# Scores in pieces of 32 columns, one projection per unit, and a reordered tail in a recurrent-then-attention kernel

## The chip, the cores and the metric

The kernel runs on one core of one Trainium2 chip, in one launch. Its metric is device time in microseconds (us), the median of several executions; beside it there is one profiled execution, from which every instruction's start and duration come. A core has a matrix engine (TensorE, PE in the profile, with its weight loads as PEld), a vector engine (VectorE, DVE), a scalar engine (ScalarE, ACT), GpSimd (POOL), and a queue engine (SyncE, SP). They run side by side and wait for one another through semaphores; DMA transfers are issued from SP, POOL and ACT.

## The reference

`x` is (2, 2048, 256), float32. Two layers are added to it, each on the layer-normalised input.

```python
# layer 1: a recurrence over time
xi = layernorm(x) @ Wi.T + bi
h_t = tanh(xi_t + h_(t-1) @ Wh.T + bh)          # 2048 steps, width 256
x = x + h
# layer 2: attention with gated experts, H = 8 heads of DH = 64, E = 5 experts, 2 selected
y  = layernorm(x)
q, k = y @ Wq, y @ Wk                             # per head 2048 x 64
wv = topk_mask(y @ Ws, 2) * sigmoid(y @ Ws)       # which experts make v, with weights
v  = einsum('bthe,btek->bhtk', wv, y @ Wv)
attn = softmax(q @ k.T / 8) @ v                   # 2048 x 2048 scores for each batch and head
out = einsum('bthe,bthk,ekd->btd', topk_mask(y @ Wd, 2), attn, Wo)
x = x + out
```

Sixteen attention heads (2 batches of 8) are computed, each with 2048 x 2048 scores. All of it is float32. A float32 matmul of the program appears in the profile as two weight loads and two matmuls, called its two passes below.

## The kernel before

**Stages.** The recurrence takes the first 130 us. What follows is attention, from about 131 us to 1542 us, and a tail that `drain` writes out by hand, to 1604 us.

**Units and tiles.** `heads` lists 16 pairs (batch, head). A head is worked on in four *units* of QB = 512 queries (n = 0 to 3; `units` lists all 64). The 2048 keys of a head are 8 tiles, and a tile `t` of scores holds 2 x 128 keys by 512 queries in PSUM, two banks (`ps_s`, two buffers). The main loop runs over T; each T makes the scores of two new tiles, so a unit has U_T = 4 values of T, a head 16, and all of attention NT = 256. Products and sums of a tile follow LAG = 6 values of T later.

**One T.** The order is written out in the main loop: `exponential` of an old tile, `scores` of the two new tiles, `stage` (ACT copies a tile to SBUF), `largest` (DVE keeps the running maximum), `subtract` (the maximum is taken off, mostly by POOL, for the first tiles of a unit by DVE), the functions listed for this T in the table `before`, `products` of two old tiles (PE: exponentials times v), in some T `sums` (PE: column sums of the exponentials, with a matrix of ones), `exponential`, and the functions in the table `behind`. `fold` adds one tile to another with an accumulating DMA from POOL. Every engine works through its instructions in this order.

**Array tiles on PE.** `scores` (L635) multiplies 64 rows by 128 columns of `k` with 512 queries; its two matmuls, for o = 0 and o = 1, use the upper and the lower 64 rows of the array and write different PSUM banks, so they can run together. `products` (L715), `sums` (L736), `keys` (L140), `queries` (L159) and `project_out` (L868) use pieces of 32 columns by all 128 rows, four of which cover the array. Transposes (`turn_max`, `spread_max`, `weigh`, `turn_out`) use the whole array.

**Projections.** `keys(i, part)` and `queries(i, part)` project y to half of the keys or queries of head i: 8 matmuls (16 passes) into one PSUM buffer of the pool `misc` (two buffers), an ACT copy (L148) or scaling (L169), and for queries two DMAs on SP's queue that swap halves (L170, L171). A head needs four of them. With T0 = 16 i the first T of head i, they are put into `before` at

```python
at(before, T0 - 2 * U_T + 2, keys, i, 0)      # the head before, unit n = 2, its third T
at(before, T0 - 2 * U_T + 3, queries, i, 0)   # the head before, unit n = 2, its fourth T
at(before, T0 - U_T + 2, keys, i, 1)          # the head before, unit n = 3
at(before, T0 + 2, queries, i, 1)             # the head's own unit n = 0
```

so unit n = 2 has two projections, n = 3 and n = 0 one each, and n = 1 none. They stand between the scores and the products of their T.

**The end of a unit.** `take` (ACT L751, DVE L752) empties the single PSUM buffer `o` that `products` fills; `take_sums` does it for `d`. `close` weighs by the mask of experts, and `gather` adds the result in DRAM (`yd`). After the last head of a batch `fetch_y` brings a unit's sum back to SBUF (640 KB, SP's queue; two buffers `y`), `turn_out` transposes a block of 128 rows of it on PE and loads the residual `z` from DRAM (L860, SP's queue, three buffers), and `project_out` multiplies with Wo into a buffer `pz`, adds `z` on DVE (L876) and stores the block (L877, SP's queue).

**The tail.** In `drain` the last three units (w, v, u) are finished with the remaining blocks interleaved by hand: `turn()` and `project()` call `turn_out` and `project_out` for the next block. When it starts, the PSUM of the scores has been given to a pool of four buffers that `other` hands out; `turn_out` and `spread_max` use it there, `weigh` and `project_out` use `misc`. `close_last` ends the last unit, block by block.

Of the kernel before, what the change touches and what calls it, by code (L numbers as in the profile page):

```python
# [14 lines left out]
P = 128  # L15
# [5 lines left out]
def rnn_then_switchhead_kernel(  # L21
# [15 lines left out]
    nc = tc.nc  # L37
    B, T, D = x.shape
    E, _, DH = Wv.shape
# [80 lines left out]
    def misc(shape, nm):  # L120
        return ps_m.tile(shape, F32, tag="m", name=nm)
# [3 lines left out]
    k_of, q_of = {}, {}  # L125
# [431 lines left out]
    U_T = NCH // 4  # L557
# [71 lines left out]
    def scores(t):  # L629
        i, n = units[t // HC]  # L630
        c = t % HC
        ss = ps_s.tile([P, 2, QB], F32, tag="s", name=f"s{t}")
        for o in range(2):
            half = slice(o * DH, (o + 1) * DH)
            nc.tensor.matmul(  # L635
                ss[:, o, :],
                lhsT=k_of[i][half, c, :],
                rhs=q_of[i, n][o][half, :],
                start=True,
                stop=True,  # L640
            )
        return ss

    def stage(t, ss):
# [23 lines left out]
    def other(nm):  # L668
        return spare["pool"].tile([P, QB], F32, tag="z", name=nm)
# [8 lines left out]
    def reduce_max(u):  # L678
        pm, mq = mx_of[u]
        nc.vector.tensor_reduce(mq, pm, AX.X, ALU.max)  # L680
# [16 lines left out]
    def subtract(t, on_vector=False):  # L697
        u, c = t // HC, t % HC
        p = ring[t]
        on_vector |= c < 2  # L700
        eng, top = (nc.vector, top_of[u][0]) if on_vector else (nc.gpsimd, top_of[u][1])
        eng.tensor_tensor(p, p, top.unsqueeze(1).to_broadcast([P, 2, QB]), ALU.subtract)  # L702
# [4 lines left out]
    def products(t):  # L707
        u, c = t // HC, t % HC
        i, _ = units[u]
        if c == 0:  # L710
            o_of[u] = ps_o.tile([P, QB], F32, tag="o", name=f"o{u}")
        for o in range(2):
            for g in range(0, DH, 32):
                at_col = o * DH + g
                nc.tensor.matmul(  # L715
                    o_of[u][at_col : at_col + 32, :],
                    lhsT=v_of[i][:, 2 * c + o, g : g + 32],
                    rhs=ring[t][:, o, :],
                    start=c == 0,
                    stop=c == HC - 1,  # L720
                    tile_position=(0, at_col),
                )

    def fold(t):


        nc.gpsimd.dma_start(out=ring[t], in_=ring.pop(t + 1), accum_op=ALU.add)  # L727
# [69 lines left out]
    def fetch_y(u):  # L797

        i, n = units[u]
        b, _ = heads[i]  # L800
        y_of[b, n] = four.tile([P, QS, E, DH], F32, tag="y", bufs=2, name=f"y{b}_{n}")
        nc.sync.dma_start(out=y_of[b, n], in_=yd[b, n])

    def close_last(u, outs):

        i, n = units[u]
        b, _ = heads[i]
        po, mr = weigh(u)
        y = y_of[b, n]
        pr = four.tile([P, QS, E, DH], F32, tag="pro", bufs=1, name=f"pro{u}")  # L810
        def ready(s):
            masked(pr[:, s : s + 1], po, mr, s, 1)
            nc.vector.tensor_tensor(y[:, s], y[:, s], pr[:, s], ALU.add)

        ready(0)
        project_out(*outs[0])
        ready(1)
        project_out(*outs[1])
        for s in range(QS):
            turn_out(*outs[2 + s])  # L820
            if s + 2 < QS:
                ready(s + 2)
            if s:
                project_out(*outs[1 + s])
        project_out(*outs[-1])

    def gather(u):

# [31 lines left out]
        nc.sync.dma_start(out=z, in_=x1d[c, :, b, :])  # L860
        yT_of[b, c] = (yT, z)

    def project_out(b, c):
        yT, z = yT_of.pop((b, c))
        pz = misc([P, D], f"pz{b}_{c}")
        for k, (r0, m) in enumerate(o_chunks):
            for g in range(0, P, 32):
                nc.tensor.matmul(  # L868
                    pz[g : g + 32],
                    lhsT=yT[:, k, g : g + 32],  # L870
                    rhs=wo[:, k, :],
                    start=k == 0,
                    stop=k == len(o_chunks) - 1,
                    tile_position=(0, g),
                )
        nc.vector.tensor_tensor(z, pz, z, ALU.add)  # L876
        nc.sync.dma_start(out=out[b].rearrange("(n s) d -> s n d", s=NCH)[c], in_=z)  # L877
# [59 lines left out]
    before, first_behind, behind = {}, {}, {}  # L937

    def at(table, T, f, *a):
        table.setdefault(T, []).append(lambda: f(*a))  # L940
# [9 lines left out]
    for i, (b, h) in enumerate(heads):  # L950
        T0 = i * H_T
        if i == 0:
            at(before, 0, keys, 0, 1)
            for c in range(NCH):
                at(behind, (c + 2) // 3, first_experts, c)
        else:
            at(before, T0 - 2 * U_T + 2, keys, i, 0)
            at(before, T0 - 2 * U_T + 3, queries, i, 0)
            at(before, T0 - U_T + 2, keys, i, 1)
        at(before, T0 + 2, queries, i, 1)  # L960
        for part in range(4):
            if i == 0:
                at(behind, (3, 5, 6, 7)[part], mix, i, part)
                at(behind, (3, 5, 6, 7)[part], mix_sum, i, part)
            else:
                T = T0 + U_T * (part - 2) + 2
                at(behind, T - 2, fetch, i, part)
                at(behind, T, mix, i, part)
                at(before, T + 1, mix_sum, i, part)
        if h == H - 3 and b + 1 < B:  # L970
            for c in range(NCH):
                T = T0 + c // 2 * U_T + 1
                at(before if c % 2 else behind, T + c % 2, experts, b + 1, c)
    for b in range(1, B):

        T0 = (b - 1) * H * H_T + 2 * LAG + 3
# [22 lines left out]
    for u, (i, n) in enumerate(units):  # L999
        b, h = heads[i]  # L1000
# [3 lines left out]
        outs = [(b, n * QS + s) for s in range(QS)]  # L1004
# [19 lines left out]
    def drain():  # L1024


        w, v, u = len(units) - 3, len(units) - 2, len(units) - 1
        tv, tu = HC * v, HC * u
        outs = [(B - 1, c) for c in range(NCH)]
        turned, projected = 2, 1  # L1030

        def turn(n=1):
            nonlocal turned
            for _ in range(n):
                turn_out(*outs[turned])
                turned += 1

        def project(n=1):
            nonlocal projected
            for _ in range(n):  # L1040
                project_out(*outs[projected])
                projected += 1

        spread_max(v)
        turn_max(u)
        subtract(tv + 6, True)
        subtract(tv + 7)
        reduce_max(u)
        take_sums(w)
        exponential(tv + 5)  # L1050
        project()
        spread_max(u)
        products(tv + 4)
        products(tv + 5)
        fold(tv + 2)
        fold(tv + 4)
        exponential(tv + 6)
        exponential(tv + 7)
        subtract(tu, True)
        close(w)  # L1060
        gather(w)
        turn()
        fetch_y(v)
        exponential(tu)
        subtract(tu + 1, True)
        exponential(tu + 1)
        subtract(tu + 7)
        subtract(tu + 2, True)
        products(tv + 6)
        products(tv + 7)  # L1070
        fold(tv + 6)
        turn()
        project()
        take(v)
        sums(tv, tv + 2, True, False)
        project()
        exponential(tu + 2)
        subtract(tu + 3, True)
        exponential(tu + 3)
        subtract(tu + 4, True)  # L1080
        products(tu)
        products(tu + 1)
        turn()
        fold(tu)
        subtract(tu + 5, True)
        exponential(tu + 4)
        turn()
        project()
        products(tu + 2)
        products(tu + 3)  # L1090
        fold(tu + 2)
        sums(tv + 4, tv + 6, False, True)
        take_sums(v)
        exponential(tu + 5)
        subtract(tu + 6, True)
        turn()
        project()
        exponential(tu + 6)
        products(tu + 4)
        products(tu + 5)  # L1100
        exponential(tu + 7)
        turn()
        fetch_y(u)
        project()
        close(v)
        gather(v)
        products(tu + 6)
        products(tu + 7)
        take(u)
        project()  # L1110
        sums(tu, tu + 2, True, False)
        sums(tu + 4, tu + 5, False, False)
        sums(tu + 6, tu + 7, False, True)
        take_sums(u)
        turn()
        turn()
        project()
        turn()
        project()
        turn()  # L1120
        close_last(u, outs[-QS - 2 :])

    with tc.manual_schedule():
        for T in range(NT):
# [11 lines left out]
            ss = [scores(t) for t in new]  # L1136
# [84 lines left out]
```

## Time and profile before

| what | value |
|---|---|
| time, median of 3 | 1605.14 us (1604.32 to 1608.18) |
| the profiled execution | 1606.15 us, of which the span from the first to the last instruction is 1604.4 us |
| granted TensorE clock | 0.997 |
| PE busy | 1536.7 us, 96% |
| DVE, POOL, ACT busy | 1300.1, 1278.1, 1250.1 us (81%, 80%, 78%) |
| scores, L635 (two groups side by side) | 512.2 us each |
| products, L715 | 492.6 us |
| sums, L736 | 150.8 us |
| queries and keys, L159 and L140 | 63.3 and 61.5 us |
| DVE `largest`, L656 | 390.6 and 78.3 us |
| POOL `subtract`, L702 | 1046.6 us |

How to read it: a busy PE is not yet a PE at its peak, since a matmul's span covers its way through the array, and matmuls overlap. What a stage costs on PE is the distance from one pass's start to the next one's. Matmuls on different tiles of the array show as several records that start within hundredths of a microsecond. A wait names the engine whose signal came last. The shares are averages; what bounds a unit is read from that unit.

### The profile page before, as it was taken

How to read it: one execution, taken by the hardware profiler on the slowest of the kernel's cores; microseconds unless marked ns; L12 is line 12 of the kernel's file. 1: busy time of each engine (PE TensorE's matmuls, PEld its weight loads, DVE VectorE, ACT ScalarE, POOL GpSimd, SP SyncE). 2: the span in 40 equal slices, each digit the busy share in tenths (PEclk: the TensorE clock that was granted, in tenths of full speed). 3: DMA queues.
4: the chain of work that ended last, by engine and by line, in shares of the span. 5: the costliest groups of instructions: out<-in, count | busy, mean ns of one | idle time of the engine just before them, and what ended most of it. 6: DMA issues, size and time to landing. Idle time of an engine off the chain costs nothing.

```text
span 1604.4 us, 29221 instructions
## 1 busy us (share of the span) xinstructions
PE 1536.7 (96%) x11438; PEld 592.6 (37%) x11438; DVE 1300.1 (81%) x1811; ACT 1250.1 (78%) x1617; POOL 1278.1 (80%) x855
## 2 busy tenths in 40 slices
PE   7989899999999999999999999999999999999998
PEld 5974233333333333333333333333333333333233
DVE  7473889998988888888987769898889888898874
ACT  4664688888878888887877768888888888888873
POOL 3054699888888988999998768898889899888880
PEclk9999999999999999999999999999999999999999
DMA  5021468788888888788887757788888888789864
GB/s 163 1 107 31 114 151 195 162 186 178 174 164 173 171 178 174 154 176 176 166 186 163 166 137 178 173 174 173 170 166 168 173 165 180 155 171 178 177 140 128
DMA packets 86911, 253.30 MB, mean 158 GB/s; under 512 B 11952, under 2 KB 31216, under 8 KB 86768
## 3 DMA queue, kind: packets, MB, share of 16 engines
q0 software_dynamic: 43488, 164.65, 54.9%
q1 hardware_dynamic: 41648, 86.13, 17.5%
q8 instruction: 91, 1.49, 0.4%
q10 hardware_dynamic: 1632, 0.61, 0.2%
q14 instruction: 52, 0.43, 0.1%
HBM read 59.46 MB, written 50.33 MB: 68 GB/s over the span
## 4 chain that ended last, share of the span: by engine, by line
PE 67%; DVE 13%; DMA 5%; ACT 3%; issue 2%; POOL 2%; SPq 0%; DVEq 0%; ACTq 0%; POOLq 0%
PE s L635 23%; PE o L715 20%; PE d L736 6%; DVE m L656 5%; DMA p<-p 4%; PE pk L140 4%; PE pq L159 3%; PE pz L868 2%; ACT p L646 2%; DVE pro L781 2%; PE pt L689 2%; PE pm L675 1%; DVE p L702 1%; POOL p L702 1%; PE po L768 1%
## 5 line engine op out<-in xcount | busy, mean ns | idle before, releaser
L702 POOL TENSOR_TENSOR p<-p,top 128x1024 f32<-128x1024 f32 x378 | 1046.6, 3007 | 11.5 <-ACT top L695 11.4
L646 ACT COPY p<-s 128x1024 f32<-128x1024 f32 x512 | 511.1, 1012 | 150.9 <-DVE m L656 69.2
L705 ACT ACTIVATE p<-p 128x1024 f32<-128x1024 f32 x512 | 538.1, 1062 | 51.0 <-DVE p L702 39.7
L635 PE MATMUL s<-qs,k 64*128 64x512 f32 x1024 | 512.2, 618 | 6.3 <-ACT p L646 6.2
L635 PE MATMUL s<-q,k 64*128 64x512 f32 x1024 | 512.2, 618 | 3.2 <-ACT p L646 3.2
L715 PE MATMUL o<-p,v 128*32 128x512 f32 x4096 | 492.6, 598 | 9.9 <-DVE os L752 8.0
L656 DVE TENSOR_TENSOR m<-s,m 128x1024 f32<-128x1024 f32 x320 | 390.6, 1221 | 95.2 <-PE s L635 86.5
L727 POOL DMA_DIRECT2D p<-p x254 | 337.3, 1329 | 69.5 <-PE o L715 21.6
L715 PEld LDWEIGHTS o<-p,v 128*32 128x32 f32 x4096 | 113.9, 109 | 298.2 <-issue 157.6
L635 PEld LDWEIGHTS s<-qs,k 64*128 64x128 f32 x1024 | 168.9, 185 | 144.7 <-ACT p L646 47.8
L635 PEld LDWEIGHTS s<-q,k 64*128 64x128 f32 x1024 | 168.9, 185 | 137.5 <-issue 52.5
L736 PE MATMUL d<-p,ones 128*32 128x512 f32 x1032 | 150.8, 593 | 5.9 <-DMA p<-p 5.8
L702 DVE TENSOR_TENSOR p<-p,pt 128x1024 f32<-128x1024 f32 x126 | 152.3, 1209 | 0.0
L656 DVE TENSOR_TENSOR m<-s,p 128x1024 f32<-128x1024 f32 x64 | 78.3, 1224 | 55.9 <-ACT p L646 55.5
L835 POOL DMA_DIRECT2D yd<-pro x48 | 45.0, 937 | 92.7 <-DVE pro L781 90.4
L781 DVE TENSOR_TENSOR pro<-po,mr 128x1280 f32<-128x1280 f32 (+1 forms) x67 | 95.9, 1431 | 2.7
L620 DVE TENSOR_TENSOR xq<-xq,wp 128x1280 f32<-128x1280 f32 x60 | 89.2, 1487 | 2.3 <-DVE wp L618 0.2
L626 DVE TENSOR_REDUCE v<-xq 128x256 f32<-128x1280 f32 x60 | 88.5, 1476 | 0.0
L736 PEld LDWEIGHTS d<-p,ones 128*32 128x32 f32 x1032 | 36.9, 110 | 96.2 <-issue 76.4
L159 PE MATMUL pq<-xn2T,wq 128*32 128x512 f32 x512 | 63.3, 612 | 6.4 <-DVE rtd L427 6.4
L140 PE MATMUL pk<-xn2T,wk 128*32 128x512 f32 x512 | 61.5, 598 | 0.0
L680 DVE TENSOR_REDUCE mq<-pm 128x4 f32<-128x512 f32 x64 | 44.3, 692 | 18.3 <-PE pm L675 16.9
(179 smaller groups left out, 1480.9 us busy)
## 6 DMA issues: line engine op xcount, KB each, us to landing
p<-p POOLq DMA_DIRECT2D x254, 512.0 KB, 6.1
xq<-xvd SPq DMA_DIRECT2D x60, 640.0 KB, 5.5
yd<-pro POOLq DMA_DIRECT2D x48, 640.0 KB, 7.2
qs<-q SPq DMA_DIRECT2D x64, 128.0 KB, 2.6
yd<-pro SPq DMA_DIRECT2D x8, 640.0 KB, 4.3
y<-yd SPq DMA_DIRECT2D x8, 640.0 KB, 6.3
x<-in_x SPq DMA_DIRECT2D x16, 256.0 KB, 5.5
x1d<-x SPq DMA_DIRECT2D x16, 256.0 KB, 2.0
```

The lines of the kernel that those rows point to most:

```text
L140: nc.tensor.matmul(pk[at_col : at_col + 32], lhsT=wk[:, kc, h * DH + g : h * DH + g + 32], rhs=xc[:, kc, c0 // 2 : (c0 + HC) // 2, o, :], ...
L159: nc.tensor.matmul(pq[at_col : at_col + 32, :], lhsT=wq[:, kc, h * DH + g : h * DH + g + 32], rhs=xn2T[:, kc, b, n * QB : (n + 1) * QB], s ...
L620: nc.vector.tensor_tensor(xq, xq, wp.unsqueeze(2).to_broadcast([P, 4, DH, E]), ALU.mult)
L635: nc.tensor.matmul(ss[:, o, :], lhsT=k_of[i][half, c, :], rhs=q_of[i, n][o][half, :], start=True, stop=True,)
L646: nc.scalar.copy(p, ss)
L656: nc.vector.tensor_tensor(m, ss, ring[t - 1] if c == 1 else m, ALU.max)
L702: eng.tensor_tensor(p, p, top.unsqueeze(1).to_broadcast([P, 2, QB]), ALU.subtract)
L705: nc.scalar.activation(ring[t], ring[t], AF.Exp)
L715: nc.tensor.matmul(o_of[u][at_col : at_col + 32, :], lhsT=v_of[i][:, 2 * c + o, g : g + 32], rhs=ring[t][:, o, :], start=c == 0, stop=c == ...
L727: nc.gpsimd.dma_start(out=ring[t], in_=ring.pop(t + 1), accum_op=ALU.add)
L736: nc.tensor.matmul(den_of[u][32 * g : 32 * (g + 1), :], lhsT=ones32, rhs=ring[(t, t1)[g // 2]][:, g % 2, :], start=first, stop=last, tile_ ...
L781: nc.vector.tensor_tensor(dst, po[:, s : s + n, 0:DH].unsqueeze(2).to_broadcast([P, n, E, DH]), mr[:, s : s + n].unsqueeze(3).to_broadcast ...
```

## The change

Four edits.

1. `scores` issues each of its two matmuls as four, of 32 columns each, with their tile position given (64 rows by 32 columns): 8 matmuls of two passes for a tile of scores in place of 2.
2. `keys(i, 0)` is put one unit earlier (the third T of unit n = 1 of the head before) and `queries(i, 0)` one T earlier (the third T of n = 2). So each unit has one projection, always in its third T.
3. In `drain`, `fetch_y(v)` stands two blocks later (after the turn of block 4), and one `project()` stands behind two more exponentials and subtractions than before.
4. `project_out` has an argument with which its PSUM buffer comes from `other`; `close_last` uses that for every second block.

```diff
@@ scores
-            nc.tensor.matmul(
-                ss[:, o, :],
-                lhsT=k_of[i][half, c, :],
-                rhs=q_of[i, n][o][half, :],
-                start=True,
-                stop=True,
-            )
+            for g in range(0, P, 32):
+                nc.tensor.matmul(
+                    ss[g : g + 32, o, :],
+                    lhsT=k_of[i][half, c, g : g + 32],
+                    rhs=q_of[i, n][o][half, :],
+                    start=True,
+                    stop=True,
+                    tile_position=(o * DH, g),
+                )
@@ close_last
-        project_out(*outs[1])
+        project_out(*outs[1], True)
...
-                project_out(*outs[1 + s])
-        project_out(*outs[-1])
+                project_out(*outs[1 + s], s % 2 == 0)
+        project_out(*outs[-1], True)
@@ project_out
-    def project_out(b, c):
+    def project_out(b, c, at_end=False):
...
-        pz = misc([P, D], f"pz{b}_{c}")
+        pz = other(f"pz{b}_{c}")[:, :D] if at_end else misc([P, D], f"pz{b}_{c}")
@@ the table of the main loop
-            at(before, T0 - 2 * U_T + 2, keys, i, 0)
-            at(before, T0 - 2 * U_T + 3, queries, i, 0)
+            at(before, T0 - 3 * U_T + 2, keys, i, 0)
+            at(before, T0 - 2 * U_T + 2, queries, i, 0)
             at(before, T0 - U_T + 2, keys, i, 1)
@@ drain
         turn()
-        fetch_y(v)
         exponential(tu)
...
         sums(tv, tv + 2, True, False)
-        project()
         exponential(tu + 2)
         subtract(tu + 3, True)
         exponential(tu + 3)
         subtract(tu + 4, True)
+        project()
         products(tu)
         products(tu + 1)
         turn()
+        fetch_y(v)
         fold(tu)
```

## The prediction, made before the changed kernel ran

> **What bounds the kernel now.** I read the page's busy times first, then the chain, then single units by windows and waits, and last the tail.
>
> ```profile
> PE 1536.7 (96%) x11438; PEld 592.6 (37%) x11438; DVE 1300.1 (81%) x1811; ACT 1250.1 (78%) x1617; POOL 1278.1 (80%) x855
> ...
> PE 67%; DVE 13%; DMA 5%; ACT 3%; issue 2%; POOL 2%; SPq 0%; DVEq 0%; ACTq 0%; POOLq 0%
> ```
>
> PE has 96% and two thirds of the chain; no other engine passes 81%. But is PE the bound in every unit? The windows of four units of one head (n = 0, 1, 2, 3 in rows; columns: length, then busy PE, PEld, DVE, ACT, POOL):
>
> ```profile
> 1043.31:1063.82 20.51, 20.51 (x144) 6.84 (x141) 18.36 (x22) 17.63 (x21) 18.76 (x12) 1.00 0.88 180
> 1063.82:1083.70 19.88, 18.83 (x128) 6.32 (x124) 18.36 (x22) 17.14 (x20) 17.95 (x12) 1.00 0.83 168
> 1083.70:1106.22 22.52, 22.52 (x160) 7.38 (x157) 20.05 (x24) 18.89 (x22) 21.16 (x15) 1.00 0.82 163
> 1106.22:1126.54 20.32, 20.32 (x145) 6.65 (x141) 16.78 (x20) 17.14 (x20) 16.39 (x11) 1.00 0.85 174
> ```
>
> PE is never idle in n = 0, 2, 3. Only n = 1, which has no projection (128 passes, against 160 in n = 2), leaves PE idle for 1.05 us. Its waits on PE:
>
> ```profile
> PE o L715 <- DVE os L752: 0.6, 1, 0.6
> PE s L635 <- ACT p L646: 0.4, 1, 0.4
> ```
>
> In its third T the products wait until DVE has emptied the one buffer `o`; in its fourth the scores wait until ACT has copied the tiles before. Now one T on PE (start, duration):
>
> ```profile
> 1063.82 0.69 PE L635 MATMUL s<-qs,k 64*128 64x512 f32 x1
> 1063.83 0.69 PE L635 MATMUL s<-q,k 64*128 64x512 f32 x1
> 1064.35 0.59 PE L635 MATMUL s<-qs,k 64*128 64x512 f32 x1
> ...
> 1064.78 0.59 PE L635 MATMUL s<-qs,k 64*128 64x512 f32 x1
> ...
> 1065.21 0.59 PE L635 MATMUL s<-qs,k 64*128 64x512 f32 x1
> ...
> 1065.74 0.66 PE L675 MATMUL pm<-ident,mm 128*128 128x128 f32 x4
> ```
>
> Passes follow at 0.43 us, both row halves together. The first takes 0.53, and it lasts 0.69 rather than 0.59: its weights load in the open. The step to the next shape of tile takes 0.53 too. A projection made of 32-column pieces shows how short the open load is there (min/median/max of a pass, ns):
>
> ```profile
> L140 PE MATMUL pk<-xn2T,wk x512: 592/592/617, 127.0 to 1456.0; 128*32 128x512 f32 x171
> ```
>
> The tail (SP's transfers, then DVE and PE):
>
> ```profile
> 1555.85 0.32 SPq L802 DMA_DIRECT2D y<-yd  x1
> 1556.27 0.97 SPq L860 DMA_DIRECT2D z<-x1d  x1
> ...
> 1562.24 0.42 DVE L876 TENSOR_TENSOR z<-pz,z 128x256 f32<-128x256 f32 x1 [3.05 <-DMA z<-x1d]
> ...
> 1565.20 1.91 PE L868 MATMUL pz<-wo,yT 128*32 128x256 f32 x24 [3.13 <-ACT yT L855]
> ```
>
> A residual of 128 KB goes out right behind the sum of 640 KB and lands at 1562.16, 5.9 us after issue; DVE stands on it for 3.05 us with subtractions queued behind, so exponentials and PE come late.
>
> **What the Trainium skill says.** "TensorEngine Tiling (Array Packing)", Key Properties: another tiling mode drains the engine, another tile does not. The trace agrees: 0.52 to 0.53 us between shapes, 0.43 within one, so 0.09 for a drain. 64x32 is as different from 128x32 as 64x128 was: no drain goes away. "TensorE: Matmul & The Clock Gate", LDWEIGHTS: a load costs by its columns, columns / 1.2 ns; by that an estimate of 107 ns for 128 and 27 for 32; the trace has 693 - 589 = 104 and 617 - 592 = 25. The same page, Part 3 (packing small matmuls), has 16 tiles of the array at work together, at about 4 ns each. The trace shows that for two tiles of 64x128 and four of 128x32, about 7 ns apart by raw starts; eight tiles of two passes each it does not show. The same page ("Wait — 56ns, not 53.3ns?") gives 62 ns per matmul where the sequencer decodes in software; in the tail 48 matmuls take 2.80 us with the last one's 0.38 us of travel, 50 ns each, so that limit isn't met here.
>
> **The change part by part.**
>
> *Scores in pieces.* Passes in time stay four for the two tiles of a T, at 0.43 us if all eight pieces run together. The entry gets shorter: 104 - 25 = 79 ns less open load. The exit gets longer: eight pieces start 7 ns apart, so the last begins 7 x 7 = 49 ns after the first, against 7; 42 ns more before the drain ends. Net about 37 to 40 ns for each T: 256 x 0.039 = 10 us, where PE bounds. Head 15's later units have no projection and wait for others, and some T wait for DMA; I take 8. Instructions rise by 3 x 2048 = 6144 matmuls and as many loads; the longest stretch, two tiles of scores, asks for 32 in 1.72 us, 54 ns each, as the tail does over 48. Bounds: -10; above, if eight pieces don't run together, see the rivals. ACT, DVE and POOL do what they did.
>
> *One projection per unit.* Nothing is added: 8 matmuls, 16 passes of 1.72 us PE time and an ACT copy of 0.59 move from n = 2 to n = 1, the query's scaling and its two DMAs one T forward. n = 2 loses 4 x 0.43 = 1.72 us of PE time that bounds it. n = 1 gains 1.72, put between scores and products of its third T, exactly ahead of the wait for `os`. Start to start that wait is 1076.72 - 1075.51 - 0.52 = 0.69 us in this head, and the scores behind it come 0.50 us late: 1.19 in all, hidden under the projection. The unit should grow by 0.53, n = 2 shrink by 1.72. The waits for `os` happen in 12 units of the whole trace; two belong to head 15's n = 1 and 2 or 3, which get no projection, so 9 or 10 heads gain 1.2 us: 11.5. Head 0, whose n = 1 idles for other reasons, gives perhaps 1.5. Sum -13. Bounds: 0 (the waits come back in another T) and -20 (all PE idle time of all n = 1 units). Queued behind the moved instructions: on ACT the next exponentials, 0.59 us in a unit with 17.14 of 19.88 busy; on SP the late layers' loads of `xl`, now behind the two `qs` transfers, with two T until use. Buffers: `k` has two and the older is free; `q` of n = 0 and 1 is last read in n = 1, before this T. So no new wait that I can see.
>
> *fetch_y(v) later, project() later.* The residual should land in the 2.0 to 2.6 us of its neighbours instead of 5.9, so DVE does not stand (3.05), nor PE (3.13 of 3.6 in all). The 640 KB then go out about 6 us later; the next residual behind it is needed over 8 us after that, and `y` itself at 1579: hidden, and if it were not, one stall of up to 3 us returns. -4; bounds -1 and -6.
>
> *pz from the other pool.* In `close_last` the second block's matmuls wait 0.81 us for DVE, since `po` and the first `pz` hold both buffers of `misc`. That goes; the end then still hangs on residual loads behind stores. -1; bounds 0 and -1.
>
> Sum: -8 - 13 - 4 - 1 = -26 us. The profiled execution is 1606.15 (span 1604.4 and 1.75 around it), 1.0 above the median; the same sum on the median: 1605.14 - 26 = 1579.
>
> **The rivals.**
>
> *Row halves don't run together* (slower). In the program the four pieces of the upper half, both passes, stand before those of the lower. To start the eighth piece PE must reach over 26 waiting instructions; for four pieces it reaches over some ten, which is all that the trace shows. If it can't, the lower half follows one pass later and each visit to the scores costs 0.43 more: 256 x 0.43 = 110, so 1579 + 8 + 110 = 1697. It decides from 0.1 us per visit (26 / 256). For it: nothing of this kind was seen in 64-row tiles. Against: short passes of 80 columns from 16 matmuls start 17 ns apart, so many instructions are ready ahead.
>
> *A pass gets slower* with eight streams: 26 us over 1024 passes is 25 ns, 6% of 0.43; at half of that 1592, at 8% 1614. Against: products keep four streams of 128 rows, the same number of reads, at 0.43.
>
> *The scores bring nothing*, since other engines set the pace once PE is faster (ACT, DVE and POOL have 17 to 19 us in a unit of 20.3): 1587.
>
> *The projection brings nothing*: the waits in n = 1 move to its first T, where POOL's subtractions sometimes hold PE: 1592.
>
> **How the numbers follow.** Likeliest case (all parts work, 1570 to 1588): 0.55. Scores nothing 0.14, projection nothing 0.09: still faster. Row halves apart 0.12. Slower passes 0.07, half of which ends above the time before. Tail worse by a collision, with little else, 0.03. Measurement tells 0.3%, 4.8 us. Faster by more: 0.55 + 0.14 + 0.09 + 0.02 = 0.80; within 0.04; slower 0.16. The range leaves out the row halves and the far low end: 1567 to 1613, which takes in the weaker cases and a pass slowed by 8%.
>
> **What would show it.** Scores: passes at 0.43 with eight starts in 0.05 us, a first pass of some 617 ns, and 0.52 after the last start to the next shape; a lower half starting 0.43 late shows the first rival. Units: n = 1 near 20.3 with PE never idle, n = 2 near 20.6, no wait for `os` in heads 1 to 14. Tail: no DVE wait of 3 us for `z`, no PE wait of 3 us for `yT`. The prediction is wrong if PE's idle time grows in units with one projection, or if groups of score pieces take over 0.45 us per pass.

## The result, and the profile after

The changed kernel takes 1592.0 us (median of 6 runs, 1589.5 to 1598.4) where the kernel before takes 1605.3 in the same session: a ratio of 0.9921, 95% interval 0.9899 to 0.9943. That is 13 us, half of the forecast 26. The profiled execution's span went from 1604.4 to 1589.5 us, at a granted clock of 0.996.

The scores on PE first. From the page, and then PE's own instructions in one T (start, duration, both in us; xN is a group that started together):

```profile
L636 PE MATMUL s<-q,k 64*32 64x512 f32 x4096 | 497.5, 596 | 2.8 <-ACT p L648 2.4
```

```profile
1049.67 0.63 PE L636 MATMUL s<-q,k 64*32 64x512 f32 x4
1049.70 0.63 PE L636 MATMUL s<-qs,k 64*32 64x512 f32 x4
1050.12 0.61 PE L636 MATMUL s<-q,k 64*32 64x512 f32 x4
...
1050.55 0.61 PE L636 MATMUL s<-q,k 64*32 64x512 f32 x4
...
1050.98 0.61 PE L636 MATMUL s<-q,k 64*32 64x512 f32 x4
...
1051.55 1.93 PE L717 MATMUL o<-p,v 128*32 128x512 f32 x16
```

The eight pieces of both row halves start together (over all passes, the last 45 to 52 ns behind the first), passes follow at 0.43 us, and the next shape begins 0.52 us after the last start. That is what was forecast. So PE's bare work did shrink: adding up passes, open loads and drains with those step lengths for attention gives 1325.5 us before and 1314.9 after. What is left of attention's time, PE standing, only went from 69.2 to 65.7.

The standing, by what PE waited for (total, times, longest), before and after:

```profile
PE s L635 <- ACT p L646: 9.3, 16, 1.7
PE o L715 <- DVE os L752: 8.0, 12, 0.7
...
PE d L736 <- DMA p<-p: 5.8, 6, 1.6
PE pt L689 <- DVE mq L680: 4.6, 10, 1.2
```

```profile
PE d L738 <- DMA p<-p: 8.6, 7, 2.9
PE pt L691 <- DVE mq L682: 6.4, 13, 1.2
...
PE s L636 <- ACT p L648: 4.3, 7, 1.3
...
PE o L717 <- DVE os L754: 1.5, 2, 0.8
```

The waits of `s`, and of `o` for `os`, fell by 11.5 us together, as forecast. But sums waiting for folds rose from 5.8 to 8.6, and `pt` from 4.6 to 6.4. The late folds cost more than these rows say: a call of `sums` has eight matmuls, 0.45 us from first start to last when nothing is missing; added over all calls the excess is 22.7 us before and 30.7 after.

The four units of a head, by time (length; PE, PEld, DVE, ACT, POOL busy; clock, DMA share, GB/s):

```profile
1033.85:1054.26 20.41, 20.41 (x240) 6.05 (x237) 18.37 (x22) 17.63 (x21) 18.71 (x12) 1.00 0.88 180
1054.26:1074.68 20.42, 20.42 (x241) 6.06 (x237) 18.37 (x22) 17.64 (x21) 18.64 (x12) 1.00 0.85 171
1074.68:1095.69 21.01, 21.00 (x241) 6.07 (x237) 18.36 (x22) 17.62 (x21) 19.22 (x12) 1.00 0.88 179
1095.69:1115.98 20.29, 20.22 (x241) 5.83 (x237) 18.36 (x22) 17.63 (x21) 17.86 (x12) 1.00 0.80 166
```

Over heads 9 to 14 the means were 21.04, 19.92, 22.40 and 20.32 us for n = 0 to 3 before, and are 20.96, 20.48, 20.75 and 20.67: n = 2 fell by 1.65 and n = 1 rose by 0.56, near the 1.72 and 0.53 forecast for the moved projections alone. The pieces should have taken 0.16 from every unit besides; n = 3 and n = 0, which only they touch, did not fall as a whole. In these heads no unit is shorter than 20.29 us, though its PE work is 19.95.

The tail gained about 1.5 us (from the first scores of the last unit to the end, 78.5 to 77.0). The stall of 3.05 us is gone, but DVE now stands three times for a residual (SP's transfers, then DVE and PE):

```profile
1549.03 1.15 SPq L862 DMA_DIRECT2D z<-x1d  x1
1550.29 0.98 SPq L804 DMA_DIRECT2D y<-yd  x1
1551.37 1.17 SPq L862 DMA_DIRECT2D z<-x1d  x1
```

```profile
1556.58 0.42 DVE L878 TENSOR_TENSOR z<-pz,z 128x256 f32<-128x256 f32 x1 [6.88 <-issue]
...
1560.91 0.42 DVE L878 TENSOR_TENSOR z<-pz,z 128x256 f32<-128x256 f32 x1 [1.96 <-DMA z<-x1d]
1563.82 0.42 DVE L878 TENSOR_TENSOR z<-pz,z 128x256 f32<-128x256 f32 x1 [2.48 <-DMA z<-x1d]
```

```profile
1561.39 0.66 PE L770 MATMUL po<-ident,os 128*128 128x128 f32 x4 [2.74 <-DVE z L878]
```

The longest stand, 6.88 us, has no engine's name in the profile ("issue"). It ends when the residual that went out at 1549.03, ahead of the sum, lands at 1556.50. The fold issued before that residual, at 1547.94, landed at 1556.28.

### The profile page after: what moved, and what is told of

It is laid out like the page before. It is cut to its first block, busy times and chain, and to the rows that moved or that the text cites. A ratio compares the mean times of both kernels' runs of the same rounds, so it can differ in the third digit from the quotient of the medians.

```text
span 1589.5 us, 41502 instructions
## 1 busy us (share of the span) xinstructions
PE 1529.4 (96%) x17582; PEld 542.1 (34%) x17582; DVE 1299.2 (82%) x1811; ACT 1248.1 (79%) x1617; POOL 1280.7 (81%) x855
## 5 line engine op out<-in xcount | busy, mean ns | idle before, releaser
L636 PE MATMUL s<-q,k 64*32 64x512 f32 x4096 | 497.5, 596 | 2.8 <-ACT p L648 2.4
L636 PE MATMUL s<-qs,k 64*32 64x512 f32 x4096 | 497.3, 596 | 2.9 <-ACT p L648 1.9
L658 DVE TENSOR_TENSOR m<-s,m 128x1024 f32<-128x1024 f32 x320 | 390.5, 1220 | 108.0 <-PE s L636 99.6
L729 POOL DMA_DIRECT2D p<-p x254 | 346.2, 1364 | 53.3 <-ACT p L707 19.8
L738 PE MATMUL d<-p,ones 128*32 128x512 f32 x1032 | 156.1, 594 | 8.6 <-DMA p<-p 8.6
L636 PEld LDWEIGHTS s<-qs,k 64*32 64x32 f32 x4096 | 102.6, 106 | 151.5 <-issue 56.7
L636 PEld LDWEIGHTS s<-q,k 64*32 64x32 f32 x4096 | 102.6, 106 | 147.8 <-issue 59.2
L658 DVE TENSOR_TENSOR m<-s,p 128x1024 f32<-128x1024 f32 x64 | 78.4, 1224 | 57.3 <-ACT p L648 56.8
L783 DVE TENSOR_TENSOR pro<-po,mr 128x1280 f32<-128x1280 f32 (+1 forms) x67 | 95.9, 1431 | 2.7
L396 POOL TENSOR_TENSOR x<-x,hvb 128x512 f32<-128x512 f32 x14 | 17.9, 1277 | 45.8 <-ACT hs L369 34.2
```

The source lines that it names most:

```text
L636: nc.tensor.matmul(ss[g : g + 32, o, :], lhsT=k_of[i][half, c, g : g + 32], rhs=q_of[i, n][o][half, :], start=True, stop=True, tile_positi ...
L658: nc.vector.tensor_tensor(m, ss, ring[t - 1] if c == 1 else m, ALU.max)
L738: nc.tensor.matmul(den_of[u][32 * g : 32 * (g + 1), :], lhsT=ones32, rhs=ring[(t, t1)[g // 2]][:, g % 2, :], start=first, stop=last, tile_ ...
L783: nc.vector.tensor_tensor(dst, po[:, s : s + n, 0:DH].unsqueeze(2).to_broadcast([P, n, E, DH]), mr[:, s : s + n].unsqueeze(3).to_broadcast ...
```

## Experiments

Ratios are to the kernel before in the same session (1606 to 1607 us), with 95% intervals.

### The parts alone

**Pieces alone**: the kernel before with edit 1 of the change.

> The kernel before with the scores in pieces alone. Theory A (once PE is a little shorter, DVE sets the length of a unit: the second tile of scores in the third T waits for the running maximum of the T before, at about 20.3 us): only n = 2 units, which are far above 20.3, get the whole 0.17 us; n = 1 stays at 19.9, n = 0 and 3 near 20.3; 3 to 5 us less than before. Rival B (PE sets every unit, and the pieces are worth their 0.04 us per T everywhere): 8 to 10 us less.

1604.9 us, ratio 0.9997 (0.9988 to 1.0005): nothing, less than either expectation. PE's bare work fell by the same 10.6 us, and its standing rose by 11.2.

**Projections alone**: edit 2.

> The kernel before with the two projections moved alone. Theory A: units of n = 1 rise to about 20.3 and n = 2 fall to about 20.7, and this edit has nearly all that the attention gained in the changed kernel: 9 to 12 us less than before. Rival B (the pieces bring 8 to 10, this edit the small rest): 3 to 5 us less.

1596.3 us, 0.9935 (0.9922 to 0.9949): 10.3 us. Standing fell from 69.2 to 56.2.

**Tail alone**: edits 3 and 4.

> The kernel before with the edits of the tail alone. If the stall on the residual behind the sum only moves to a later residual, as the trace of the changed kernel suggests, 1 to 2 us less than before, all of it from the last 15 us (the PSUM buffer); if the stall goes away, 4 to 5 us less.

1606.1 us, 0.9994 (0.9984 to 1.0004): nothing that can be told; 1.6 us in the spans of the two profiled executions.

So nearly all of the gain is the moved projection. The next question is what turns less PE work into more standing.

### Less PE work

In the changed kernel, projections from the second head on use half of the contraction (the other half of the keys' and queries' sums is left out):

```diff
-        for kc in range(KC):
+        for kc in range(1 if i else KC):
...
```

> The changed kernel with half of each projection's contraction left out from head 1 on (kc = 0 only): 0.86 us less PE work in each of 60 units, nothing taken from the other engines. Theory A: units stay at 19.9 to 20.3, so 6 to 20 us less than the changed kernel, and waits on DVE and DMA grow. Rival B: all of it is gained, 50 us.

1571.9 us, 0.9791 (0.9773 to 0.9809). Of 51.5 us of PE work taken away, 20 came off the time and 31 went into standing. Many units stop at 19.9 us, which is also the length, before, of the unit without a projection (19.88). So PE was not alone in setting the pace.

### The wide multiply on DVE, and gather

At the end of a unit DVE makes `pro` (L783, 1.49 us), ahead of two maxima and two subtractions of the next T; the second scores of the T behind that, the third of the unit, wait for one of these maxima. POOL then issues `gather`, the accumulating transfer of `pro`. Two suspects: DVE's order, and transfers. First the multiply behind those four instructions, gather left where it was:

```diff
-        masked(pr, po, mr, 0, QS)       # at the end of close(u)
+    def close_rest(u):                  # its own function
+        masked(pr, po, mr, 0, QS)
...
+            before.setdefault(T1 + LAG + 3, []).insert(0, lambda u=u: close_rest(u))
```

> The changed kernel with the wide multiply of close (1.49 us on DVE) put behind the two maxima and two subtractions of its T instead of ahead of them; no work added or left out. Theory A (DVE's row of work in the second T makes the scores of the third T late, 0.29 us in some 22 units): these waits go, units fall from 20.3 to 20.0, 5 to 8 us less than the changed kernel. Rival C (units are held by DMA landing times and anything gained is lost there): within 2 us of the changed kernel, with the waits on the folds' DMA grown.

1787.1 us, 1.112 (1.110 to 1.114). POOL's own instructions show why:

```profile
1124.95 0.88 POOL L729 DMA_DIRECT2D p<-p  x1 [0.49 <-PE o L717]
1134.56 0.87 POOL L842 DMA_DIRECT2D yd<-pro  x1 [8.72 <-DVE pro L783]
```

POOL stands at gather for `pro` 8.7 us here, 262 us in 47 places, with the next subtractions and folds queued behind. The Trainium skill's "TensorE: Matmul & The Clock Gate" (the table at its head) calls GpSimd's queue strictly first in, first out, and this trace agrees. The same wait is in the kernel before and in the changed kernel:

```profile
POOL yd L835 <- DVE pro L781: 90.4, 42, 3.1
```

```profile
POOL yd L837 <- DVE pro L783: 87.8, 42, 3.3
```

**Gather left out** (the changed kernel, for the six of eight heads that use this line; the sums over heads are not formed):

```diff
-            nc.gpsimd.dma_start(out=yd[b, n], in_=pr, accum_op=ALU.add)
+            pass
```

> The changed kernel with the accumulating transfers of gather left out (six heads of eight, 640 KB in each of 48 units), so that the folds land sooner. Theory A: the waits of sums on the folds fall from 8.6 us to some 3, units of n = 1 to 3 stay at 20.3 because DVE still sets them; 3 to 8 us less than the changed kernel. Rival C (DMA is what took the gain): 10 us or more less, with units at 20.0.

1567.4 us, 0.9762 (0.9747 to 0.9777), 25 below the changed kernel. All but one of the units of heads 9 to 14 take 20.30 us: neither expectation had that much gain at that length. **The same in the kernel before**:

> The kernel before, with the accumulating transfers of gather left out for heads 1 to 6 of 8 in each batch (the sums over heads 2 to 7 are not formed; everything else runs). The same edit took 24.6 us from the changed kernel (1567.4). Theory: late folds held up the faster PE of the changed kernel more than the slower one of before, so here the edit brings only 10 to 16 us (1590 to 1596), and without these transfers the change as a whole is worth the forecast 23 to 29 us. Rival: gather costs every kernel of this kind the same, about 24 us: 1581, and the change is worth 13 us with or without it.

1590.8 us, 0.9901 (0.9887 to 0.9915), 16 below. Without gather the change is worth 23 us, with it 13. But this edit takes away 640 KB a unit and POOL's stand together. Two runs separate them. **Thin transfers** (32 KB; most of the sums are not formed), POOL still standing:

```diff
-            nc.gpsimd.dma_start(out=yd[b, n], in_=pr, accum_op=ALU.add)
+            nc.gpsimd.dma_start(
+                out=yd[b, n][:, 0:1, 0:1], in_=pr[:, 0:1, 0:1], accum_op=ALU.add
+            )
```

> The changed kernel, with gather of heads 1 to 6 adding only one block's first 64 columns in place of all 1280 (the sums over heads are not formed in the rest): 32 KB in place of 640 KB, while POOL still stands at gather for the wide multiply. Leaving the transfers out altogether gave 1567.4. Theory traffic: 1566 to 1572. Theory POOL's stand: 1586 to 1592. Both in part: in between.

1590.2 us, 0.9895 (0.9875 to 0.9915): with 5% of the bytes, as slow as the changed kernel. The stand is still there:

```profile
POOL yd L837 <- DVE pro L783: 87.3, 42, 3.3
```

**Gather one T later** (but not in the last head of a batch), all bytes moved:

```diff
-            at(behind, T1 + LAG + 3, gather, u)
+            at(behind, T1 + LAG + (3 if h == H - 1 else 4), gather, u)
```

> The changed kernel with gather issued one T later for all heads but the last of a batch, and nothing else moved: all bytes stay, but POOL no longer stands 1.8 us a unit for the wide multiply. Theory traffic: 1588 to 1593, unchanged. Theory POOL's stand: 1568 to 1576.

1574.9 us, 0.9799 (0.9785 to 0.9812): 17 us below the changed kernel from this line alone, and faster than both kernels. It isn't the traffic; it is POOL's stand. POOL's instructions in the changed kernel:

```profile
1062.23 0.87 POOL L837 DMA_DIRECT2D yd<-pro  x1 [1.78 <-DVE pro L783]
1062.80 2.71 POOL L704 TENSOR_TENSOR p<-p,top 128x1024 f32<-128x1024 f32 x1
1065.16 1.19 POOL L729 DMA_DIRECT2D p<-p  x1
...
1082.63 0.87 POOL L837 DMA_DIRECT2D yd<-pro  x1 [1.79 <-DVE pro L783]
```

and with the later gather:

```profile
1060.85 0.88 POOL L729 DMA_DIRECT2D p<-p  x1 [0.55 <-issue]
1061.46 2.70 POOL L704 TENSOR_TENSOR p<-p,top 128x1024 f32<-128x1024 f32 x1
1063.80 1.21 POOL L837 DMA_DIRECT2D yd<-pro  x1
```

In the first, POOL works without a gap from one gather to the next, 20.40 us of which it stands 1.79, and the fold behind gather goes out 2.93 us after it. Counted from DVE's start on `pro` (1058.17 in the second trace; 1080.84, less a unit of 20.40, in the first), that fold leaves after 4.72 us in the first and 2.68 in the second. So this fold leaves 2 us late, and the others of the unit by up to 0.7. With the later gather the excess in `sums` falls from 30.7 to 7.7 us, of which 5.6 is one call at 821 us, in the last head of the first batch, where gather keeps its place; every unit of heads 9 to 14 takes 20.30. The folds also land sooner, in a median 5.8 us in place of 6.6, but that isn't the cause: with the thin transfers they land in 5.9, and the excess stays at 29.1. Leaving gather out altogether is worth 7.5 us more than moving it (1567.4); nearly 6 of that is excess in `sums`, most of it that one call.

### The floor of 20.30 us

What holds a unit at 20.30, when its PE work is 19.95? Weight loads of the second scores in the third T, in the run with the later gather:

```profile
1063.11 0.13 PEld L636 LDWEIGHTS s<-qs,k 64*32 64x32 f32 x5 [0.99 <-DVE m L658]
```

The first scores of this T start at 1061.93 and take two passes, 0.46 and 0.43 us, so PE comes 0.29 us late here, in each unit: it waits for the DVE maximum (L658) that frees the scores' buffer. **The multiply later, this time with gather later too** (for all heads but the last of a batch):

```diff
-                at(behind, T1 + LAG + 3, gather, u)
+                before.setdefault(T1 + LAG + 3, []).insert(0, lambda u=u: close_rest(u))
+                at(behind, T1 + LAG + 4, gather, u)
```

> The changed kernel, where DVE's wide multiply at a unit's end (L783, 1.49 us) follows the two maxima and subtractions of its T in place of standing ahead of them, and gather comes one T later. The second scores of that T then need not wait for a maximum, and POOL does not stand at gather. All bytes are still moved. Theory 1 (DVE's order holds the unit at 20.30, traffic makes folds late): the waits of scores for a maximum go, units fall to 20.0 to 20.2, the waits of sums for transfers stay: 1583 to 1589. Theory 2 (POOL standing at gather makes folds late, not traffic): sums do not wait either, 1568 to 1576. Rival: whatever is freed is lost to later folds: 1590 to 1594.

1650.8 us, 1.028 (1.0265 to 1.0296): no expectation had that, and POOL still stands at gather, 63.1 us in 41 places. Without gather, and so without that stand, it is the same (1653.3, 1.0291, 1.0277 to 1.0304), so something else sets the pace here:

> The order of the run before this one, with the accumulating transfers of gather left out for heads 1 to 6 (sums over heads not formed). Set beside it, this takes away the bytes alone, since POOL does not stand at gather in either. Theory 1 (traffic): 15 to 22 us below that run, 1562 to 1568, with units under 20.30. Theory 2 (POOL's stand was the cause): no more than 5 us below that run.

The multiply now stood ahead of DVE's half of `take` (L754), and the products after it were late: the wait of `o` for `os` rose to 12.7 us in 41 places. That is a part of the loss only. **Behind `take`**, gather behind that:

```diff
-                before.setdefault(T1 + LAG + 3, []).insert(0, lambda u=u: close_rest(u))
-                at(behind, T1 + LAG + 4, gather, u)
+                before.setdefault(T1 + LAG + 4, []).insert(0, lambda u=u: close_rest(u))
+                at(behind, T1 + LAG + 5, gather, u)
```

> The later wide multiply again, but now behind DVE's half of take (L754) as well, which stood behind it in the run of 1650.8 and came 1.5 us late there with all products after it. Gather follows one T behind the multiply. Theory 1 (DVE's order in the second T holds the unit at 20.30): no scores wait for a maximum, units of 19.95 to 20.15, 1580 to 1588. Rival (other engines or late folds hold the unit as well): units stay at 20.3, 1589 to 1594.

1655.2 us, 1.0298 (1.0283 to 1.0313). That wait is gone, but units take 20.61 us in heads 9 to 14: the scores of the first T are 0.38 late each time. Most of the loss, 66 of 80 us against the run with gather alone later, is in heads 3 to 8, where the second batch's work runs as well. There PE's waits ahead of tiles in the two-buffer pool `misc` add up to 46 us, against 3.6 in that run; a multiply that comes later also holds its `po` in that pool longer. That this is the cause was not tested. With the fetch of the next section added, these orders give 1651.2 and 1653.3.

> The two single gains together: the later wide multiply and gather, and fetch_y(v) right behind the turn of block 3 (worth 3 us alone). If they add up: 3 us below the kernel with the later multiply, 1580 to 1586 by theory 1. If the later multiply brings nothing: 1589, as with the fetch alone.

> The order of the run before this one, and fetch_y(v) right behind the turn of block 3, worth 3 us alone. If the gains add up: 3 us below that run. If the earlier ends of units change what the fetch meets, the same as that run.

So neither later place for the multiply was cheap, and that the maximum sets the floor remains a reading of the trace. What PE's own speed does to the floor was tried directly: **the kernel before with the moved projections and the later gather**, whole scores:

> The kernel before with the moved projections and gather one T later, scores in whole matmuls and the old tail. The changed kernel with the later gather took 1574.9. Theory (the pieces' 8 us are real and were lost because POOL's stand at gather made folds late; the tail edits are worth about 1): 1583 to 1587, units of 20.3 to 20.7. Rival (pieces bring nothing whatever POOL does): 1575 to 1578.

1576.1 us, 0.9814 (0.98 to 0.9827); the same with pieces and the new tail took 1574.9, and the intervals overlap. The pieces bring nothing here either. One unit of each (whole scores, then pieces; columns as above):

```profile
1062.90:1083.21 20.31, 20.31 (x143) 6.65 (x141) 18.36 (x22) 17.63 (x21) 18.64 (x12) 1.00 0.87 169
```

```profile
1063.11:1083.41 20.30, 20.22 (x236) 5.81 (x236) 18.36 (x22) 17.63 (x21) 18.78 (x12) 1.00 0.84 169
```

Bare PE work, added up as above, is 20.12 and 19.95 us, and the unit is the same. The trace with pieces shows a circle of waits. Here are DVE and ACT in the run with the later gather:

```profile
1069.76 1.23 DVE L658 TENSOR_TENSOR m<-s,m 128x1024 f32<-128x1024 f32 x1 [0.66 <-PE s L636]
...
1076.71 1.23 DVE L658 TENSOR_TENSOR m<-s,p 128x1024 f32<-128x1024 f32 x1 [0.78 <-ACT p L648]
...
1082.14 1.22 DVE L658 TENSOR_TENSOR m<-s,m 128x1024 f32<-128x1024 f32 x1
```

```profile
1071.06 1.01 ACT L648 COPY p<-s 128x1024 f32<-128x1024 f32 x1 [0.52 <-ACT p L648]
...
1074.75 1.93 ACT L648 COPY p<-s 128x1024 f32<-128x1024 f32 x2
```

PE's second scores of the third T start at 1063.11. By 1069.76 PE has made the fourth T's scores and DVE takes their maximum. ACT's copy follows that at 1071.06, and ACT works without a gap to 1076.68. There DVE goes on, `pro` among its work, without a gap to 1083.36, and PE's second scores of the next unit start at 1083.41. Of 20.30 us, PE has 6.65; the projection lies in that stretch, which fits the shorter units, 19.9, with half a projection or none. With whole scores that stretch is 6.66 (1062.90 to 1069.56). In pieces its last pass does start 0.12 earlier (5.90 us into the stretch against 6.02), but the last of eight starts 0.04 later behind the first than the last of two, and DVE begins 0.11 after its end in place of 0.05. What pieces save elsewhere lies outside the circle. That the circle holds the unit is read from these traces; that the pieces bring nothing is measured.

### The tail

`fetch_y(v)` between its two places, right behind the turn of block 3:

```diff
         turn()
+        fetch_y(v)
         project()
         take(v)
...
         turn()
-        fetch_y(v)
         fold(tu)
```

> The changed kernel with the sum of the last unit but one fetched right behind the turn of block 3, between the place that it had before the change and the one after it: ahead of it are the residuals of blocks 2 and 3, behind it none until block 4. If the stall is a residual queued behind the sum, both the 3 us of before and the 2.7 us of after go: 2 to 3 us less than the changed kernel. If the folds alone make residuals late: no change.

1589.0 us, 0.9896 (0.9879 to 0.9914); that interval overlaps with the changed kernel's. In this run the sum has landed (1548.15) before the residual goes out (1548.46), and still that residual takes 7.0 us and DVE stands 6.4 us for it; it lands 0.23 us behind the fold issued before it, as in the changed kernel (0.22). So the late residual goes with the folds ahead of it, not with the sum. With the later multiply of the run of 1787: 1784.2, 1.110 (1.108 to 1.112).

> Both moves together, each independent of the other: the sum of their gains, 7 to 11 us less than the changed kernel by theory A, 2 to 3 by rival C.

With the later gather:

> The changed kernel with gather one T later (1574.9 alone) and fetch_y(v) right behind the turn of block 3 (3 us alone). One lies in the units, the other in the tail, so they should add up: 1570 to 1574. If the earlier fetch only collides with other transfers: 1575.

1575.6 us, 0.9801 (0.9786 to 0.9816), as without it (1574.9). The fetch in between is not shown to bring anything.

## Why the prediction was half right

**Scores in pieces, -8: wrong, they bring nothing.** The eight streams, the open load and the drain were as forecast, and so was the 10 us of PE work. The step that failed is "256 x 0.039 = 10 us, where PE bounds": PE was taken to bound nearly every T. But in a unit with one projection PE's bare work, 20.12 us, already lies 0.19 below the 20.31 at which a circle over PE, DVE and ACT holds the unit, so a shorter PE only stands longer. The rival "the scores bring nothing" came nearest, with a chance of 0.14; it named the busy time of the other engines, where the traces show a circle of waits. The profile of before had a sign of it: its n = 3, with one projection and 100% of PE busy, took 20.32 us, and n = 1, without one and with 5% of PE idle, 19.88. A busy share of 100% was taken for PE at its limit. The prediction's own sign of being wrong came too: over heads 9 to 14, n = 3 went from 20.32 to 20.67 us though its PE work had shrunk.

**One projection per unit, -13: the mechanism was right, the size 10.3 alone.** Waits for `os` and for `s` behind them fell by 11.5 us. Without POOL's stand the same move takes the time from 1590.8 to 1576.1, 14.7 us (a rough figure, since the first of the two also lacks gather's bytes); with it, part goes into late folds.

**"ACT, DVE and POOL do what they did", and "So no new wait that I can see": the omission.** POOL stood 1.8 us a unit at gather for a multiply on DVE, in the kernel before too. With units of 20.3 us it then works without a gap, so its folds leave late, and a faster PE waits for them: 22.7 us before, 25.8 with the projection alone, 30.7 with both. With gather later, 7.7 are left. The forecast looked for new waits among buffers and queues that the edit touches, and didn't ask who is late next once PE arrives earlier everywhere.

**Tail, -4 and -1: 1.6 in the spans of these edits alone.** The step that failed is "The residual should land in the 2.0 to 2.6 us of its neighbours": the three around the sum land 7.5, 9.4 and 6.2 us after their issue, the first of them ahead of the sum and close behind a fold. DVE's waits that the profile names as waits for a residual rose from 6.4 to 9.4 us in the tail, and the 6.88 without a name come on top; the prediction's "one stall of up to 3 us returns" was too small. The gain lies at the end, which fell from 16.1 to 14.7 us from the last `den` on.

That 1592 lies inside the stated 1567 to 1613 is owed to the room left for weaker cases. Of the 13 us that are missing, about 8 are the pieces, and the projection and the tail share the rest.

Row halves did run together and no pass got slower, so these rivals fell.

## To carry over

When an engine shows 100% busy, compare units that differ in its work alone: if the time doesn't follow the work, a circle of waits over other engines sets the pace, and a faster form of instruction brings nothing. Before making the busiest engine faster, look at every in-order queue for an instruction that stands for another engine, and price what is queued behind it. Moving such an instruction behind the point where its input is ready can be worth more than the speed-up: here 17 us for one line, against 13 for four edits.

## What was not expected of the hardware

- Eight streams of 64 x 32, two passes each, start 6.7 ns apart, the last 45 to 52 ns behind the first, although in program order both passes of the upper half's pieces stand before the lower half. (The very first piece of attention, at 132.01 us, shows that order: it went alone, and its second pass followed 0.45 us later, while the next piece came at 134.01.) So starts on different array tiles are not in program order. "TensorE: Matmul & The Clock Gate", Part 3 (packing small matmuls), says matmuls start in strict order without reordering; here the measurement differs.
- While POOL stood ahead of its issue, an accumulating transfer of 640 KB or of 32 KB in each unit, with DMA engines 80 to 90% busy, made a difference of 2 us in 1592, within what the runs scatter; the wait ahead of the issue made 17.
